# A window-attention layer and three convolution layers: the input laid out ahead of the launch, and the intermediate tensor stored in the layout of its readers

## The chip, the cores and the metric

The kernel runs on one core of a Trainium2 chip. The metric is the device time of one execution in microseconds. Its engines, as the profile names them: PE (TensorE, with PEld for its weight loads), DVE (VectorE), ACT (ScalarE), POOL (GpSimd) and SP (SyncE, which here only issues DMAs). Sixteen DMA engines move the data.

## The reference

The input x has 4 images of 16 channels and 512 x 512 pixels in float32. Four layers follow each other, all with 16 channels in and out:

```python
# layer 0: depthwise 3x3 convolution added to x, then attention in 8x8 windows, then an MLP
x = x + depthwise3x3(x, pos_w) + pos_b
win = windows(x * alpha1 @ color1 + beta1)          # 64 tokens of 16 channels
q, k, v = win @ qkv_w.T + qkv_b                     # 2 heads of 8 channels
x = x + proj(softmax(q * 8**-0.5 @ k.T) @ v)
x = x + fc2(gelu(fc1(x)))                           # 16 -> 64 -> 16
# layer 1: x and weights rounded to 8 bits by their largest value, 3x3 convolution,
#          normalised by mean and variance over all images and pixels, clipped to [0, 6]
# layer 2: x + conv3x3(relu(conv3x3(x, w1) + b1), w2) + b2
# layer 3: x + w2 @ relu(w1 @ conv3x3(x) + b1) + b2 # 16 -> 128 -> 16
```

Two things in it divide the work into stages. Layer 1 can round only when the largest value of all of layer 0's output is known, and it can normalise only when mean and variance of its whole convolution are known. So the output of layer 0 goes to DRAM and is read twice: once for the statistics and once for the real work.

## The kernel before

**Layer 0** is `window_attention`. A tile `x{k}` holds one row of windows (8 pixel rows and a border row above and below) by 128 columns, of 8 strips of each of the 4 images: 128 partitions are image, strip parity and channel (32 b + 16 w + c), and `V = 4` pairs of strips lie along the free dimension. There are 32 such tiles and 64 steps of 64 columns (`STEPS`). `load(k)` (line 271 ff.) brings a tile in with 32 DMAs, one for each image, strip parity and strip pair, each of 16 partitions with 10 rows of 129 or 130 floats; GpSimd sets the borders of the picture to zero. `depthwise` (L297) multiplies it by nine diagonal matrices `taps` (made on DVE at L246 from the constant `hot`), `position` writes the result `y`, and `turn_keys` (L320) transposes blocks of `y` between partitions by 32 DMAs a step into `y2`. `values` (L348), `scores` (L361), `attend` and `divide` are the attention, `project`, `hidden` (L418) and `output` (L431) the rest. In step n, TensorE works on the depthwise convolution of step n + 2 and the hidden layer of step n, and SyncE turns the keys of step n + 1. After each odd step `store` (L447) writes four blocks `xo[:, u]` to DRAM, each with 8 DMAs; `load` of the tile after next is called after each even step. `xo` has one buffer, x tiles two.

The order of PE, DVE, ACT and SP inside layer 0 and inside the convolutions is the order of the program (`tc.manual_schedule`); SP issues its DMAs strictly in that order, and each of its DMAs uses one of eight semaphores in turn, so it waits for the DMA eight places earlier. What stands ahead of the schedule (weights, folding, first constants) is ordered by the framework's scheduler.

At the end of layer 0 a bound on the scores is computed; every engine reads the flag and branches (L133, L539) around `attention_block`, a slower version of layer 0 which doesn't run for this input.

**Layers 1 to 3** are `conv_layers`. Here a tile `tx{mm}` holds one pair of rows of each of four strips (S = 4) of each image: partition is 32 b + 16 (row of the pair) + c, and the free dimension is strip by 512 columns. `_load_pairs` (L898) gathers it from x1 with four DMAs, one for each image, in runs of one row of 512 floats. For mm below 0 or above M = 64 one strip lies outside the picture and is set to zero by DVE. The **statistics pass** goes through the 64 tiles: DVE scales (L990), ACT rounds to bfloat16 (L993), TensorE convolves with the rounded weights (L914), DVE takes the statistics of the four banks (L1015). Loads run four tiles ahead, in four slots; rounding runs two ahead. Then the tiles come a second time, and all four convolutions and layer 3's hidden layer run in one software pipeline, one row pair a turn, in which `turned` (L1101) copies blocks between partitions.

**The tensor between them**, x1, has the shape [image, row + 1, channel, column]; a row of zeros is written above and below each picture at the start (L112, L113).

Of the kernel before, what the change touches and what calls it, by code (L numbers as in the profile page):

```python
# [11 lines left out]
F32 = mybir.dt.float32  # L12
# [11 lines left out]
B, C, H, W = 4, 16, 512, 512  # L24
P = 128
HR = H // 2
WP = W + 2
NS = 8
S = 4
M = H // S // 2  # L30
NH, HD = 2, 8
WS = 8
# [51 lines left out]
        nc.sync.dma_start(part[:, at : at + m, :], src[:, a : a + m, :])  # L84


def _store_rows(nc, dst, src, r0, n):
    for half in range(2):
        a = half * HR + r0 + 1
        for b in range(B):  # L90
            at = 64 * half + C * b
            nc.sync.dma_start(
                dst[b, a : a + n].rearrange("r c w -> c r w"), src[at : at + C]
            )


def _pad_columns(nc, t):
# [1 line left out]


@with_exitstack
def conv_chain(ctx: ExitStack, tc: tile.TileContext, x, mats, vecs, cqs, cws, hots, out):
    nc = tc.nc
    const = ctx.enter_context(tc.tile_pool(name="const", bufs=1))
    dram = ctx.enter_context(tc.tile_pool(name="dram", bufs=1, space=DRAM))


    x1 = dram.tile([B, (S + 1) * 2 * M, C, W], F32, name="x1")
    zero = const.tile([C, W], F32, name="zero")
    nc.vector.memset(zero, 0.0)  # L110
    for b in range(B):
        nc.sync.dma_start(x1[b, 0], zero)  # L112
        nc.sync.dma_start(x1[b, H + 1], zero)  # L113

    mat = const.tile([P, N_MAT], F32, name="mat")
    vec = const.tile([P, N_VEC], F32, name="vec")
    cw = const.tile([P, 3, 2, 3, 32], F32, name="cw")
    nc.sync.dma_start(mat, mats)
    nc.sync.dma_start(vec, vecs)
    nc.scalar.dma_start(cw, cws)  # L120

    def m(name):
        return mat[:, MAT_AT[name]]

    def v(name):
        return vec[:, VEC_AT[name]]

    cq, sw = quant_weights(tc, const, cqs)
    peak = const.tile([P, 4 * HR // WS], F32, name="peak")
    nc.gpsimd.memset(peak, 0.0)  # L130

    safe = window_attention(tc, x, x1, hots, m, v, peak)
    with tc.If(safe == 0):  # L133
        attention_block(tc, x, x1, m, v, peak)
    conv_layers(tc, x1, out, cw, cq, sw, m, v, peak)


@with_exitstack
def window_attention(ctx: ExitStack, tc, x, x1, hots, m, v, peak):

# [10 lines left out]
    nc = tc.nc  # L153
    U = V = 4
# [3 lines left out]
    XW = 2 * BW  # L158
    SR = H // 8
    NQ = W // XW  # L160
# [11 lines left out]
    def quad(i):  # L172
        return slice(32 * i, 32 * i + 32)

    hot = wts.tile([P, 64], F32, name="hot")
    nc.sync.dma_start(hot, hots)
    small, own = hot[:, 0:32], hot[:, 32:64]
# [70 lines left out]
    px = ctx.enter_context(tc.tile_pool(name="w0x", bufs=2))  # L248
# [8 lines left out]
    g = pa.tile([P, V, NJ, NH, T], F32, name="g")  # L257
    o = pa.tile([P, V, NJ, NH, T], F32, name="o")
    most = pa.tile([P, STEPS], F32, name="most")

    def load(k):
        i, cb = divmod(k, NQ)
        t = px.tile([P, V, WS + 2, XW + 2], F32, tag="x", name=f"x{k}")
        if cb == 0:
            nc.gpsimd.memset(t[:, :, :, 0:1], 0.0)
        if cb == NQ - 1:
            nc.gpsimd.memset(t[:, :, :, XW + 1 : XW + 2], 0.0)
        if i == 0:
            nc.gpsimd.memset(t[:, 0, 0, :], 0.0)
        if i == SR // WS - 1:  # L270
            nc.gpsimd.memset(t[:, V - 1, WS + 1, :], 0.0)
        c0, c1 = max(0, XW * cb - 1), min(W, XW * cb + XW + 1)
        at = c0 - XW * cb + 1
        for b in range(U):
            for w in range(2):
                for vv in range(V):
                    r = SR * (2 * vv + w) + WS * i - 1
                    r0, r1 = max(0, r), min(H, r + WS + 2)
                    nc.sync.dma_start(
                        t[32 * b + C * w : 32 * b + C * w + C, vv, r0 - r : r1 - r,  # L280
                          at : at + c1 - c0],
                        x[C * b : C * b + C, r0:r1, c0:c1],
                    )
        return t

    def by_window(ap):
        return ap.rearrange("p (j a x) -> p a j x", a=WS, x=WS)
# [150 lines left out]
    def store(xo, k, u):  # L438
        i, cb = divmod(k, NQ)
        nc.vector.tensor_reduce(  # L440
            peak[:, U * k + u : U * k + u + 1], xo[:, u], AX.XY, ALU.max,
            apply_absolute_value=True,
        )
        for vv in range(V):
            for w in range(2):
                r = SR * (2 * vv + w) + WS * i
                nc.sync.dma_start(  # L447
                    x1[u, r + 1 : r + 1 + WS, :, XW * cb : XW * cb + XW].rearrange(
                        "a c x -> c a x"
                    ),  # L450
                    xo[32 * vv + C * w : 32 * vv + C * w + C, u],
                )

    ctx.enter_context(
# [4 lines left out]
            }  # L459
        )  # L460
    )
    xts, ys = {0: load(0), 1: load(1)}, {}
    for n in range(2):
        for tap in range(9):
            for u in range(U):
# [6 lines left out]
    last, xo = None, None  # L472
    for n in range(STEPS + 1):
# [32 lines left out]
        if n % 2 == 0:  # L506
            xo = px.tile([P, U, WS, XW], F32, tag="xo", name=f"xo{n}", bufs=1)
# [35 lines left out]
def attention_block(ctx: ExitStack, tc, x, x1, m, v, peak):  # L543
# [3 lines left out]
    nc = tc.nc  # L547
# [7 lines left out]
    px = ctx.enter_context(tc.tile_pool(name="l0x", bufs=2))  # L555
# [54 lines left out]
    for i in range(2):  # L610
        t = wts.tile([P, CJ, 4, 2 * C], F32, name=f"vals{i}")
# [137 lines left out]
    def mlp_hidden(xw, n, k, g):  # L749
        xc = chunk(xw, k)  # L750
        ph = psT.tile([P, 4, P], F32, tag="t", name=f"ph{n}_{g}")
        ph = ph.rearrange("p a b -> p (a b)")
        nc.tensor.matmul(
            ph, fc1[32 * g : 32 * g + 32], xc[32 * g : 32 * g + 32], start=True, stop=True
        )
        hid = pa.tile([P, N], F32, tag="hid", name=f"hid{n}_{g}", bufs=3)
        nc.scalar.activation(hid, ph, AF.Gelu, bias=f1b)
        return hid
# [12 lines left out]
    def mlp(xw, i):  # L771

        xo = px.tile([P, WS, W], F32, tag="xo", name=f"xo{i}", bufs=1)
        hids, todo = [], [(k, g) for k in range(NC) for g in range(4)]
        for t in range(len(todo) + 1):
            if t < len(todo):
                k, g = todo[t]
                hids.append(mlp_hidden(xw, f"{i}_{k}", k, g))
            if t:
                k, g = todo[t - 1]  # L780
                if g == 0:
                    pf = psG.tile([P, 512], F32, tag="g", name=f"pf{i}_{k}")
                nc.tensor.matmul(
                    pf[32 * g : 32 * g + 32], m("fc2"), hids.pop(0), start=True, stop=True
                )
                if g == 3:
                    mlp_out(xw, xo, pf, f"{i}_{k}", k)
        nc.vector.tensor_reduce(
            peak[:, i : i + 1], xo, AX.XY, ALU.max, apply_absolute_value=True
        )  # L790
        _store_rows(nc, x1, xo, i * WS, WS)

# [7 lines left out]
    xin, xws, qks, es, ets, os = {0: load(0)}, {}, {}, {}, {}, {}  # L802
# [13 lines left out]
    for at in range(NU + 5):  # L816
        if 0 <= at - 2 < NU:
            _, _, u, n = unit(at - 2)
            ets[at - 2] = turn(es.pop(at - 2), n, u)
        if 0 <= at - 1 < NU:  # L820
            _, _, u, n = unit(at - 1)
            normalise(es[at - 1], n, u)
        if at < NU:
            i, k, u, n = unit(at)
# [3 lines left out]
            if at + 2 < NU:  # L828
                i, k, _, _ = unit(at + 2)
# [5 lines left out]
        if 0 <= at - 3 < NU:  # L835
            i, k, u, n = unit(at - 3)
# [3 lines left out]
        if 0 <= at - 4 < NU and (at - 4) % 4 == 3:  # L840
            i, k, _, n = unit(at - 4)
# [4 lines left out]
        if at < NU:  # L846

            i, k, u, _ = unit(at)
# [36 lines left out]
def _quad(i):  # L885
    return slice(32 * i, 32 * i + 32)


def _load_pairs(nc, t, x1, mm):


    s0, s1 = int(mm < 0), S - int(mm > M)
    if s1 - s0 < S:
        nc.vector.memset(t[:, 0 if mm < 0 else S - 1, :], 0.0)
    at = 2 * M * s0 + 2 * mm
    for b in range(B):
        rows = x1[b, at : at + 2 * M * (s1 - s0)]
        nc.sync.dma_start(  # L898
            t[_quad(b), s0:s1],
            rows.rearrange("(s r) c w -> s r c w", r=2 * M)[:, 0:2].rearrange(  # L900
                "s r c w -> (r c) s w"
            ),
        )


def _turns():
# [316 lines left out]
def _pack(a):  # L1223
# [7 lines left out]
    for w in range(2):  # L1231
# [3 lines left out]
    parts = {  # L1235
        "color1": _diagonal(a["L0_conv_color1"], NS),
        "color2": _diagonal(a["L0_conv_color2"], NS),
        "wq": _diagonal(qkv_w[0].T, NS),
        "wk": _diagonal(qkv_w[1].T, NS),
        "wv": _diagonal(qkv_w[2].T, NS),  # L1240
        "proj": _diagonal(a["L0_conv_proj_w"].T, NS),
        "fc1": np.tile(fc1, (4, 1)),
        "fc2": _diagonal(a["L0_conv_fc2_w"].T, 2),
# [26 lines left out]
    mats = np.concatenate([parts[name] for name, _ in _MATS], axis=1)  # L1270
    vecs = np.concatenate([parts[name] for name, _ in _VECS], axis=1)


    cws = np.zeros((2, C, 4, 2, 3, 2, C), np.float32)
    for i, name in enumerate(
        ("L2_conv_w1", "L2_conv_w2", "L3_conv_conv_w", "L1_conv_weight")
    ):
        w = a[name].transpose(1, 2, 3, 0)
# [6 lines left out]
    cws = np.tile(cws.reshape(32, 4, 2, 3, 32), (4, 1, 1, 1, 1))  # L1285

    own = np.zeros((2, 64, 2, C))
    for w in range(2):
        own[w, :, w, :] = 1.0
    hots = np.concatenate(  # L1290
        [np.tile(np.eye(32), (4, 1)), own.reshape(P, 32)], axis=1
    ).astype(np.float32)
    return {
        "x": a["x"].reshape(B * C, H, W),
        "mats": mats,
        "vecs": vecs,
        "cqs": cws[:, 3].reshape(P, 6 * 32),
# [26 lines left out]
```

## Time and profile before

| | |
|---|---|
| median of 3 runs | 6786.55 us (6781.14 to 6790.85) |
| span of the profiled run | 6787.2 us |
| PE busy | 6456.3 us, 95% |
| ACT, DVE busy | 4215.1 us (62%), 3196.5 us (47%) |
| DMA, mean rate | 76 GB/s, 514.79 MB |
| HBM read, written | 225.28 MB, 134.48 MB |
| loads of a layer 0 tile | 1024 DMAs of about 81 KB |
| stores of layer 0 | 1024 DMAs of 64 KB |
| loads of layers 1 to 3 | 528 DMAs of 256 or 192 KB |

A page of the profile gives the busy time of each engine, then the span in 40 slices (a digit is the busy share of a slice in tenths; PEclk is the clock that TensorE was granted; GB/s is what the DMA engines moved). Further views of the same trace are used below: busy time by stretch, the instructions of one engine in order of time (start, length, engine, line, operation, output<-inputs, and in brackets the idle time ahead and what ended it), and waits by who waited for whom. In the chain that ended last, followed back from the end, only the convolution stage appears (9688 pieces, nearly all TensorE): it reaches back to about 4007 us. What lies before has to be read from the stretches.

The stages by the trace: start until 88 us, layer 0 until 3628 us, statistics pass from 3638 to 3981 us, convolutions to the end.

### The profile page before, as it was taken

Reading aid. Unit: us, or ns where it says so; the run is one execution under the profiler, and the core shown is the slowest. Engines: PE = TensorE matmul, PEld = TensorE weight load, DVE = VectorE, ACT = ScalarE, POOL = GpSimd, SP = SyncE. Lnnn points to the kernel's source line nnn. Section 1 sums busy time; section 2 is a strip of 40 time slices with the busy share of each in tenths; the row PEclk is TensorE's granted clock in tenths of the full one; section 3 lists DMA queues with packets and bytes.
Section 4 is the critical chain, followed back from the end, with each engine's and each line's share of the span. In section 5 each row is a group of like instructions: output and inputs, shape, how many; then the busy total and the mean of one; then the engine's idle time right before and its main releaser. Section 6 shows DMA issues by size and latency. Waiting matters only on the chain. (4 is left out here: it accounts for less than half of the span.)

```text
span 6787.2 us, 317928 instructions
## 1 busy us (share of the span) xinstructions
PE 6456.3 (95%) x146976; PEld 3304.6 (49%) x146976; DVE 3196.5 (47%) x4640; ACT 4215.1 (62%) x5738; POOL 10.3 (0%) x49
## 2 busy tenths in 40 slices
PE   7999999999999999999995569999999999999999
PEld 4555555555555555555552334444444444444443
DVE  2444444444444444444444764444444444444444
ACT  3777777777777777777774344555555555555553
POOL 0000000000000000000000000000000000000000
PEclk9999999999999999999996679999999999999999
DMA  6454555545454545455526962222222222322221
GB/s 72 63 66 65 63 69 63 70 61 69 63 66 62 66 63 66 64 63 68 62 43 131 212 137 72 77 77 78 83 79 78 79 79 79 82 79 78 78 62 46
DMA packets 759438, 514.79 MB, mean 76 GB/s; under 512 B 354128, under 2 KB 648656, under 8 KB 749904
## 3 DMA queue, kind: packets, MB, share of 16 engines
q1 hardware_dynamic: 757808, 493.95, 42.6%
q8 instruction: 1154, 18.91, 1.3%
q14 instruction: 188, 1.54, 0.1%
q10 hardware_dynamic: 288, 0.39, 0.0%
HBM read 225.28 MB, written 134.48 MB: 53 GB/s over the span
## 5 line engine op out<-in xcount | busy, mean ns | idle before, releaser
L1123 PE MATMUL tb<-y,mat 32*32 32x512 f32 x16384 | 1682.9, 597 | 10.4 <-ACT hid L1129 7.5
L1129 ACT ACTIVATE hid<-tb,vec 128x512 f32<-128x512 f32 x1280 | 877.9, 687 | 1229.8 <-PE tb L1123 1207.7
L369 ACT ACTIVATE e<-pair 128x1024 f32<-128x1024 f32 x1024 | 992.4, 1021 | 231.4 <-PE pair L361 230.8
L1131 DVE TENSOR_SCALAR hid<-tb,vec 128x512 f32<-128x512 f32 x768 | 576.6, 751 | 1168.1 <-PE tb L1123 852.8
L297 PE MATMUL pair<-x,taps 32*32 32x512 f32 x18432 | 1005.3, 605 | 35.0 <-issue 20.7
L418 PE MATMUL bank<-y,fc_e 32*32 32x512 f32 x8192 | 890.9, 609 | 10.4 <-issue 6.3
L423 ACT ACTIVATE hid<-bank,f1b 128x512 f32<-128x512 f32 x1024 | 679.6, 686 | 338.3 <-PE bank L418 319.1
L353 DVE COPY yt<-bank 128x512 f32<-128x512 f32 x512 | 353.7, 691 | 906.1 <-PE bank L348 905.8
L1123 PEld LDWEIGHTS tb<-y,mat 32*32 32x32 f32 x16384 | 503.7, 103 | 393.8 <-issue 231.8
L361 PE MATMUL pair<-g,y 32*128 32x128 f32 x16384 | 653.2, 285 | 40.7 <-ACT e L369 36.8
L914 PE MATMUL tb<-z,cw 32*32 32x512 f32 x12864 | 641.3, 602 | 3.5 <-ACT z L1060 2.7
L914 PE MATMUL tb<-q,cq 32*32 32x512 bf16 x12672 | 468.2, 483 | 185.0 <-issue 130.8
L914 PE MATMUL tb<-x,cw 32*32 32x512 f32 x12480 | 635.2, 598 | 1.7 <-ACT z L1060 1.5
L361 PEld LDWEIGHTS pair<-g,y 32*128 32x128 f32 x16384 | 540.3, 187 | 189.3 <-ACT e L369 107.5
L914 PE MATMUL tb<-h,cw 32*32 32x512 f32 x12672 | 628.2, 601 | 1.6 <-ACT z L1060 1.5
L297 PEld LDWEIGHTS pair<-x,taps 32*32 32x32 f32 x18432 | 447.7, 103 | 362.9 <-issue 244.1
L380 PE MATMUL bank<-e,yt 128*32 128x128 f32 x16384 | 555.5, 276 | 1.0 <-ACT r L395 0.9
L385 PE MATMUL bank<-e,hot 128*32 128x512 f32 x4096 | 534.4, 592 | 0.0
L1137 PE MATMUL tb<-hid,mat 128*32 128x512 f32 x4096 | 495.9, 602 | 0.9 <-DVE o L1143 0.9
L380 PEld LDWEIGHTS bank<-e,yt 128*32 128x32 f32 x16384 | 417.7, 109 | 108.5 <-DVE yt L353 52.8
L993 ACT ACTIVATE q<-tx,unround 128x512 bf16<-128x512 f32 (+1 forms) x333 | 313.8, 967 | 235.4 <-DVE tx L990 131.9
L431 DVE TENSOR_TENSOR xo<-bank,y 128x512 f32<-128x512 f32 x256 | 177.0, 691 | 563.8 <-PE bank L429 562.4
(154 smaller groups left out, 6542.0 us busy)
## 6 DMA issues: line engine op xcount, KB each, us to landing
tx<-x SPq DMA_DIRECT2D x520, 256.0 KB, 5.8
y<-y SPq DMA_DIRECT2D x2048, 32.0 KB, 2.1
x<-xo SPq DMA_DIRECT2D x1024, 64.0 KB, 2.1
xi<-x SPq DMA_DIRECT2D x1024, 64.0 KB, 2.6
out_dram<-o SPq DMA_DIRECT2D x64, 1024.0 KB, 4.3
x<-in_x_dram SPq DMA_DIRECT2D x496, 81.2 KB, 6.3
x<-in_x_dram SPq DMA_DIRECT2D x496, 80.6 KB, 6.4
tx<-x SPq DMA_DIRECT2D x8, 192.0 KB, 3.8
```

Of the source, the lines that this page charges most:

```text
L297: nc.tensor.matmul(bank(u)[quad(vv)], taps[quad(u), tap, :], xts[n // 2][quad(u), vv, dy : dy + WS, at : at + BW], start=tap == 0, stop=ta ...
L361: nc.tensor.matmul(bank(u)[:, P * jj : P * jj + P], y2[quad(u), vv, jl + jj].rearrange("p w t -> p (w t)"), g[quad(u), vv, jl + jj].rearra ...
L369: nc.scalar.activation(e[:, 2 * i : 2 * i + 2].rearrange("p u j t -> p u (j t)"), pairs[i], AF.Exp,)
L380: nc.tensor.matmul(b[quad(u), P * jj : P * jj + P], yt[:, jj, quad(u)], e[:, u, jj, :], start=True, stop=True,)
L385: nc.tensor.matmul(d[quad(u)], own, e[:, u].rearrange("p j t -> p (j t)"), start=True, stop=True,)
L418: nc.tensor.matmul(b[quad(k)], fc1[quad(vv), quad(k)], y[quad(vv), u, :], start=True, stop=True,)
L423: nc.scalar.activation(hd, b, AF.Gelu, bias=f1b)
L914: nc.tensor.matmul(p[i][_quad(j)], weights[_quad(i), side, dx, :], src[side][_quad(i), j, dx : dx + W], start=side == 0 and dx == 0, stop= ...
L1123: nc.tensor.matmul(p[_quad(c)], w1[_quad(b), 1 - par, 32 * c : 32 * c + 32], inner(ys(mm + par))[_quad(b), s, :], start=True, stop=True,)
L1129: nc.scalar.activation(hd, p, AF.Relu, bias=v("l3_b1"))
L1131: nc.vector.tensor_scalar(hd, p, v("l3_b1"), 0.0, ALU.add, ALU.max)
L1137: nc.tensor.matmul(out_bank[_quad(b), :], w2[:, par], hd, start=par == 0, stop=par == 1)
```

## The change

Two things are done to the layout of data in DRAM, and one to the order of the first transfers.

The input of layer 0 is laid out ahead of the launch (in `_pack`, with the arrays that hold the weights): xw holds each of the 32 tiles complete, borders and zeros included, so `load` becomes one DMA of 128 partitions with 5200 contiguous floats each, and GpSimd's memsets go. The tile pool moves in front, and the first two loads are written in front of the constant `hot` and all the weight folding. x itself stays as an input for `attention_block`.

x1 gets the layout of the later tiles, [pair, partition, strip, column]. A tile is then one contiguous block of 1 MiB, and `_load_pairs` becomes one DMA (two for the tile mm = M). In exchange the stores of layer 0 have to part even from odd rows: `_store_block` writes two DMAs where there was one, and three where a strip ends and the pair that straddles two strips belongs to the next one.

```diff
+def _store_block(nc, x1, src, b, r0, cols):
+    n = WS // 2
+    s, m = divmod(r0 // 2, M)
+    parts = [(1, m, s, 0, n), (0, m + 1, s, 0, n)]
+    if m + n == M and s < S - 1:
+        parts[1:] = [(0, m + 1, s, 0, n - 1), (0, 0, s + 1, n - 1, 1)]
+    for r, mm, ss, at, k in parts:
+        part = 32 * b + C * r
+        nc.sync.dma_start(
+            x1[mm : mm + k, part : part + C, ss, cols].rearrange("m c x -> c m x"),
+            src.rearrange("c (m r) x -> c m r x", r=2)[:, at : at + k, 1 - r],
+        )
...
-    x1 = dram.tile([B, (S + 1) * 2 * M, C, W], F32, name="x1")
+    x1 = dram.tile([M + 1, P, S, W], F32, name="x1")
...
+    xin = ctx.enter_context(tc.tile_pool(name="w0i", bufs=2))
+    def load(k):
+        t = xin.tile([P, V, WS + 2, XW + 2], F32, tag="x", name=f"x{k}")
+        nc.sync.dma_start(t, xw[k])
+        return t
+    xts, ys = {0: load(0), 1: load(1)}, {}
     hot = wts.tile([P, 64], F32, name="hot")
     nc.sync.dma_start(hot, hots)
...
-    def load(k):
-        i, cb = divmod(k, NQ)
-        t = px.tile([P, V, WS + 2, XW + 2], F32, tag="x", name=f"x{k}")
...
-        for b in range(U):
-            for w in range(2):
-                for vv in range(V):
-                    r = SR * (2 * vv + w) + WS * i - 1
-                    r0, r1 = max(0, r), min(H, r + WS + 2)
-                    nc.sync.dma_start(
-                        t[32 * b + C * w : 32 * b + C * w + C, vv, r0 - r : r1 - r,
-                          at : at + c1 - c0],
-                        x[C * b : C * b + C, r0:r1, c0:c1],
-                    )
...
                 r = SR * (2 * vv + w) + WS * i
-                nc.sync.dma_start(
-                    x1[u, r + 1 : r + 1 + WS, :, XW * cb : XW * cb + XW].rearrange(
-                        "a c x -> c a x"
-                    ),
-                    xo[32 * vv + C * w : 32 * vv + C * w + C, u],
+                _store_block(
+                    nc, x1, xo[32 * vv + C * w : 32 * vv + C * w + C, u], u, r,
+                    slice(XW * cb, XW * cb + XW),
                 )
...
-    xts, ys = {0: load(0), 1: load(1)}, {}
...
 def _load_pairs(nc, t, x1, mm):
-    s0, s1 = int(mm < 0), S - int(mm > M)
...
-    at = 2 * M * s0 + 2 * mm
-    for b in range(B):
-        rows = x1[b, at : at + 2 * M * (s1 - s0)]
-        nc.sync.dma_start(
-            t[_quad(b), s0:s1],
...
+    if mm < 0:
+        nc.vector.memset(t[:, 0], 0.0)
+        nc.sync.dma_start(t[:, 1:S], x1[M + mm, :, 0 : S - 1])
+    elif mm < M:
+        nc.sync.dma_start(t, x1[mm])
+    else:
+        nc.sync.dma_start(t[:, 0 : S - 1], x1[mm - M, :, 1:S])
+        if mm == M:
+            nc.sync.dma_start(t[:, S - 1], x1[M, :, S - 1])
+        else:
+            nc.vector.memset(t[:, S - 1], 0.0)
```

## The prediction

> **What bounds the kernel now.** I read the slices of the span first: they show where TensorE is not the bound. Each of the 40 is about 170 us.
>
> ```profile
> PE   7999999999999999999995569999999999999999
> PEclk9999999999999999999996679999999999999999
> DMA  6454555545454545455526962222222222322221
> GB/s 72 63 66 65 63 69 63 70 61 69 63 66 62 66 63 66 64 63 68 62 43 131 212 137 72 77 77 78 83 79 78 79 79 79 82 79 78 78 62 46
> ```
>
> PE is full except in the first slice and in slices 22 to 24, where DMA reaches its highest share and its highest rate. The busy time by stretch, for the three stages:
>
> ```profile
> core 0: us, PE busy (x) PEld busy (x) DVE busy (x) ACT busy (x) POOL busy (x), PEclk, DMA share, GB/s
> 2000.00:3000.00 1000.00, 980.38 (x21498) 556.59 (x21477) 453.88 (x597) 762.95 (x1016) 1.10 (x6) 1.00 0.53 65
> 3700.00:3900.00 200.00, 107.55 (x3840) 65.10 (x3823) 144.04 (x198) 78.20 (x39) 0.00 (x0) 0.62 1.00 211
> 5000.00:6000.00 1000.00, 1000.00 (x23725) 442.88 (x23727) 481.13 (x764) 506.76 (x764) 0.00 (x0) 1.00 0.29 79
> ```
>
> Layer 0 (98% PE) and the convolution stage (100% PE) are TensorE's; a transfer made cheaper there hides behind matmuls. The statistics pass of layer 1 is different: PE 54%, DVE 72%, ACT 39%, DMA 1.00. It is bound by its loads. Then the start, in SyncE's timeline:
>
> ```profile
> 7.62 0.42 SPq L119 DMA_DIRECT2D vec<-in_vecs_dram  x1
> 10.57 0.35 SPq L176 DMA_DIRECT2D hot<-in_hots_dram  x1
> 24.97 49.54 SPq L279 DMA_DIRECT2D x<-in_x_dram  x64
> 74.96 51.32 SPq L320 DMA_DIRECT2D y<-y  x64
> ```
>
> The 64 loads of the first two tiles wait until 24.97 (on DVE's weight folding) and then hold the queue for 49.54 us; the turns of the first keys stand behind them. PE in the same time:
>
> ```profile
> 31.41 4.34 PE L297 MATMUL pair<-x,taps 32*32 32x512 f32 x8 [6.90 <-DMA x<-in_x_dram]
> ...
> 50.97 9.75 PE L297 MATMUL pair<-x,taps 32*32 32x512 f32 x161 [2.05 <-DMA x<-in_x_dram]
> ...
> 66.64 6.05 PE L297 MATMUL pair<-x,taps 32*32 32x512 f32 x153 [0.88 <-ACT y L308]
> ...
> 88.45 1.11 PE L348 MATMUL bank<-mat,y 128*128 128x128 f32 x4
> ```
>
> It starts at 31.41, stops three times for pieces of x until 50.97, and reaches the first transposes of the attention loop at 88.45. From there it is full.
>
> [...]the packet records give a median of 161 ns for the 2 KiB packets of the statistics loads (12.7 GB/s an engine), 229 ns for the 6016-byte packets of the weights load (26 GB/s) and 314 ns for the 8 KiB packets of the output stores (26 GB/s).[...]
>
> **The change, part by part.**
>
> *Statistics loads.* Four DMAs of 256 KB in 2 KiB runs become one of 1 MiB in 8 KiB runs. From the first scaling at 3645.75 to the end of the last BATCH_NORM at 3980.74 the pass takes 335 us for 64 tiles, 5.2 us each; 1 MiB at 211 GB/s is 5.0 us. The new load: each of 16 engines has 8 packets of 8 KiB. At 314 ns that is 2.5 us a tile[...]. What takes over? Where the loads happened to be early, VectorE's timeline shows the pace without them:
>
> ```profile
> 3802.33 2.49 DVE L1015 BATCH_NORM_STATS2 stats<-tb 128x6 f32<-128x512 f32 x4
> 3804.74 1.27 DVE L990 TENSOR_SCALAR tx<-tx,inv_x 128x2048 f32<-128x2048 f32 x1
> 3806.03 2.49 DVE L1015 BATCH_NORM_STATS2 stats<-tb 128x6 f32<-128x512 f32 x4
> 3808.43 1.27 DVE L990 TENSOR_SCALAR tx<-tx,inv_x 128x2048 f32<-128x2048 f32 x1
> ```
>
> No idle time stands between them: 3.70 us a tile, and VectorE is the new bound (ACT needs 2.0, PE 2.8 at half clock). [...]four tiles are in flight, so the load hides. The pass becomes 64 x 3.70 = 237 us, plus 10 us of ramp (scaling 1.3, rounding twice 2.0, matmuls 2.8, waits): 247. That gives **88 us**. The first tile lands about 4.9 us after its issue (2.5 of data, and the 2.1 us to landing that the smallest issues of the page show) instead of 7.5: 2.6 more. Together **-90 us**, between -60, if bubbles stay, and -95.
>
> *First loads.* Two DMAs of 2.66 MB with a 20.8 KB run for each partition, in SyncE's order between vec and hot. At 26 GB/s on 16 engines a tile takes 6.4 us; issued at 8 and 8.5, both are in by about 22; at half that rate, by 34. Hot (the source of taps) queues behind them and lands with the second. The order of VectorE's instructions moves too: the nine taps operations now all stand after the folding that ends at 24.9, so their wait holds up nothing but themselves. Nine at 0.23 us end at 27; PE can begin at about 26 instead of 31.41, and then has no DMA waits. From 50.97, when the data was there, to 66.64 the first block took 15.7 us; then 21.8 from 66.64 to 88.45. So 26 + 15.7 + 21.8 = 63.5, against 88.45: **-25 us**. I take -24[...] and keep -12 (slow loads) to -30. The turns may start at once, at about 43; eight take 6.4 us (51.32 / 64 each), before the 63 at which they are needed.
>
> *Loads inside layer 0.* 32 issues become one, and the packets of 516 and 520 bytes (88 ns) go; GpSimd's 24 memsets of borders go. All of it lies beside a PE that is 98% busy: nothing.
>
> *Stores of layer 0.* Eight a call become 16 of half the size with the same 512-byte packets; in the bottom row of windows 19, since three strips of eight split once more. SyncE's stores of one pair of steps took 0.475 us an issue, and a zero row of 16 packets takes 0.47 as well: the cost is by issue, not by bytes. In a pair of steps of 110 us the queue has 32 + 64 + 32 = 128 issues now and 1 + 64 + 64 = 129 after. Behind the stores stand the turns of the next step: the stores of 1069.67 to 1089.1 would run to 1103, the turns to 1129, with the next step not before 1142. The slot xo is wanted again at about 1123. Nothing on PE moves. But **the last step has nothing behind which to hide**:
>
> ```profile
> 3609.06 21.99 SPq L447 DMA_DIRECT2D x<-xo  x32
> 3638.26 61.84 SPq L898 DMA_DIRECT2D tx<-x  x55
> ```
>
> VectorE has the flag at 3628.5, SyncE ends its stores at 3631.05, and the next stage loads 7.2 us later, after the branch and the stores' landing. With 76 stores of 0.475 from 3609.06 SyncE ends at 3645.2: **+14 us** on the path (+9 if the smaller stores issue in 0.41).
>
> *Convolution stage.* Four loads a tile become one; PE is at 100%. Nothing. The two memsets of the last tile's strip move; 0.5 us each, hidden.
>
> Sum: 6786.6 - 90 - 24 + 14 = 6686.6; I say **6686**.
>
> **The rivals.** (1) The pass stays at its pace, because something else than the packet size holds it: SyncE's waits in the pass are mostly for a free slot (ACT's rounding), and PE's clock of 0.62 could be the cause rather than the result of waiting. Then only the ends change: 6786.6 - 24 + 14 = 6777. Against it stands the stretch above at 3.70 us a tile; it ran with early loads and a halved clock. (2) Half the gain: VectorE and PE alternate with gaps, some 4.4 us a tile, 282 + 10 us, a gain of 43: 6786.6 - 46 - 24 + 14 = 6731. Stretches of the pass with PE waits of 5.8 us speak for it; they follow late loads, which speaks against. (3) Slower: the new stores step 1 MiB from row pair to row pair. They are 131,072 packets of 512 bytes, 46 ns each at the median now. If that pitch made them eight times as long (370 ns), they would need 131,072 x 0.37 / 16 = 3030 us of the engines, with the turns' 262,144 packets at 28 ns (459 us) and the loads (205 us) some 3690 us, more than layer 0's 3540: +150, for 6786.6 - 90 - 24 + 14 + 150 = 6837. [...]against it the DMA share of 0.53 with half of it to spare.
>
> **How the numbers follow.** The forecast 0.80, the half gain 0.09, the unmoved pass 0.06, the slower case 0.05. The unmoved pass lies within 0.2% (13.6 us) of 6786.6. Faster 0.89, same 0.06, slower 0.05. Range: for the forecast alone, -95 - 30 + 9 gives 6671 and -60 - 12 + 16 gives 6731; the half gain ends there too. I widen a little below, since the ramps are estimates: 6660 to 6735.
>
> **What would show it.** Right: the pass at about 250 us, VectorE there without idle time and DMA's share near a half; the first transposes (in the place of line 348) at 60 to 70 us; SyncE's last store of layer 0 about 19 us behind the last output in place of 5; layer 0's step still some 54 us. Wrong: ACT's rounding still waiting for loads, 8 KiB reads above 450 ns, PE waiting for turned keys, or a DMA share of layer 0 above its 0.53.

## The result, and the profile after

After: **6615.97 us** (median of 4 runs, 6611.96 to 6621.86) against 6787.35 before (4 runs, 6781.14 to 6790.85); ratio 0.9749, interval 0.9732 to 0.9766. That is 171 us less. The forecast was 100 us less, with a range that ended at 6660.

The slices of the page after the change, to be held against those of before (tenths of 40 equal slices; GB/s is what the DMA engines moved):

```profile
PE   8999999999999999999996689999999999999998
...
DMA  3333232333333333333324722222222222222221
GB/s 81 65 67 76 57 75 59 73 60 72 60 72 60 72 61 70 62 70 62 70 44 165 275 85 79 79 79 76 76 78 78 78 78 75 75 79 79 79 63 47
```

TensorE's hole around slices 22 to 24 is shallower and shorter, the highest rate rises from 212 to 275 GB/s, and DMA's share in layer 0 falls from about 5 tenths to 3. The busy time by stretch, with the columns that the prediction's view of the same kind names:

```profile
2000.00:3000.00 1000.00, 988.42 (x21859) 570.83 (x21832) 464.81 (x610) 777.44 (x1036) 0.00 (x0) 1.00 0.32 66
...
3650.00:3750.00 100.00, 67.11 (x2652) 39.24 (x2652) 99.25 (x138) 54.99 (x28) 0.00 (x0) 0.73 0.82 293
```

In layer 0 TensorE is busy 988 us of 1000, where it was 980: that line was expected to stand still. In the statistics pass VectorE is busy 99 us of 100. The start, first on SyncE, then on TensorE (start, length, engine, line, operation; in brackets the idle time before and what ended it):

```profile
7.76 0.90 SPq L194 DMA_DIRECT2D x<-in_xw_dram  x2
```

```profile
24.64 11.38 PE L295 MATMUL pair<-x,taps 32*32 32x512 f32 x288 [0.60 <-DVE taps L269]
37.27 11.71 PE L295 MATMUL pair<-x,taps 32*32 32x512 f32 x288 [1.25 <-ACT y L306]
...
55.22 1.11 PE L346 MATMUL bank<-mat,y 128*128 128x128 f32 x4
```

The two loads are issued at 7.76, TensorE's two depthwise blocks run without a stop, and the first transposes stand at 55.22 (before: 88.45). The seam behind layer 0 on SyncE, 76 stores and then the next stage's first load:

```profile
3516.80 38.39 SPq L96 DMA_DIRECT2D x<-xo  x76
3559.76 37.05 SPq L891 DMA_DIRECT2D tx<-x  x13
```

Put side by side, in us of the profiled executions (the reduction named is the `most` of each step):

| part | before | after | difference | forecast |
|---|---|---|---|---|
| start to the first of the 64 reductions | 108.3 | 75.4 | -32.9 | -24 |
| first to last reduction: layer 0's loop | 3472.4 | 3411.7 | **-60.7** | **0** |
| last reduction to the next stage's first load: the seam | 57.5 | 72.7 | +15.2 | +14 |
| that load to the first scaling | 7.5 | 5.0 | -2.5 | -2.6 |
| statistics pass | 335.0 | 238.7 | -96.3 | -88 |
| the rest (convolution) | 2806.4 | 2814.0 | +7.5 | 0 |

The seam is as forecast. The rest is about scatter: in the eleven experiments that leave the pass and the convolution alone, the same work took 2807.5 to 2813.6. What has to be explained is the loop, and then why start and pass gave more than their terms.

### The profile page after: what moved, and what is told of

Its sections match the earlier page's. It is cut to its first block, busy times and chain, and to the rows that moved or that the text cites. A ratio compares the mean times of both kernels' runs of the same rounds, so it can differ in the third digit from the quotient of the medians.

```text
span 6617.5 us, 317160 instructions
## 1 busy us (share of the span) xinstructions
PE 6388.5 (97%) x146976; PEld 3295.4 (50%) x146976; DVE 3192.7 (48%) x4640; ACT 4209.4 (64%) x5738; POOL 5.9 (0%) x25
## 3 DMA queue, kind: packets, MB, share of 16 engines
q8 instruction: 1154, 18.91, 1.2%
## 5 line engine op out<-in xcount | busy, mean ns | idle before, releaser
L295 PE MATMUL pair<-x,taps 32*32 32x512 f32 x18432 | 968.1, 606 | 1.9 <-ACT y L306 1.3
L908 PE MATMUL tb<-q,cq 32*32 32x512 bf16 x12672 | 446.5, 436 | 122.1 <-ACT q L987 97.9
L378 PEld LDWEIGHTS bank<-e,yt 128*32 128x32 f32 x16384 | 417.7, 109 | 108.1 <-DVE yt L351 52.8
L346 PEld LDWEIGHTS bank<-mat,y 128*128 128x128 f32 x2048 | 215.2, 141 | 430.2 <-issue 376.5
```

Of the source, the lines that this page charges most:

```text
L295: nc.tensor.matmul(bank(u)[quad(vv)], taps[quad(u), tap, :], xts[n // 2][quad(u), vv, dy : dy + WS, at : at + BW], start=tap == 0, stop=ta ...
L378: nc.tensor.matmul(b[quad(u), P * jj : P * jj + P], yt[:, jj, quad(u)], e[:, u, jj, :], start=True, stop=True,)
L908: nc.tensor.matmul(p[i][_quad(j)], weights[_quad(i), side, dx, :], src[side][_quad(i), j, dx : dx + W], start=side == 0 and dx == 0, stop= ...
```

## What the two traces show of the loop

In the trace before, an even step of layer 0 took 56.08 us and an odd one 54.13; after, 54.18 and 54.13. So 1.9 us went from each even step, the one in which x is loaded. By rows of groups over most of the loop (busy us, mean ns, then idle us before and what ended it), before:

```profile
L297 PE MATMUL pair<-x,taps 32*32 32x512 f32 x17568 | 951.2, 603 | 17.0 <-issue 16.7
...
L418 PE MATMUL bank<-y,fc_e 32*32 32x512 f32 x7808 | 848.9, 597 | 6.4 <-issue 6.3
```

and after:

```profile
L295 PE MATMUL pair<-x,taps 32*32 32x512 f32 x17624 | 932.5, 603 | 0.0
...
L416 PE MATMUL bank<-y,fc_e 32*32 32x512 f32 x7960 | 852.4, 600 | 2.0 <-ACT hid L421 1.6 <-DVE y L407 0.4
```

These are the depthwise matmuls and the hidden layer's. Before, TensorE stood 17.0 + 6.4 us ahead of them, ended by "issue": nothing that the profile knows as a wait. After, "issue" is gone from both rows. The page of before names the traffic concerned in its table of queues (packets, MB, share of the engines):

```profile
q8 instruction: 1154, 18.91, 1.3%
```

1154 packets of 16 KB. TensorE executes 293,952 matmuls and weight loads, and with the semaphore instructions among them 295,025, or 256 for each packet: these packets are its instructions, in **blocks of 256**. I number them all in the order of their starts, take the number modulo 256, and call the time from one start to the next a gap. Of the 24 gaps above 1 us in the loop before the change, 21 fall on one and the same value, 193 (the other three lie in the last step). The gaps at that value sum to 63.5 us, where a value's median is 13.4. After, it has 10.7 us, and the median is 8.8. So 52.8 of the 60.7 us lie there; the rest is spread over other places. And each of the 21 gaps ends 1.5 to 2 us after one of these packets has landed. From this I read that TensorE ran out of instructions. Normally (the median after the change) the packet of the next block starts 0.5 us into the present block and lands at 1.6; ahead of the 21 gaps it landed 3.6 to 5.4 us into its block.

## The experiments

The first four test a first version of this theory (A: the small packets of the old loads hold the instruction packets back) and two rivals (B: the stores, or GpSimd's border memsets; C: the number of issues on SyncE). The last column of this table is the sum of gaps at the block boundaries of the loop.

| run | loads of x; when they are issued, us into the even step | loop | gaps at boundaries | time (median) | ratio to before |
|---|---|---|---|---|---|
| before | 32; 19 to 42 | 3472.4 | 63.5 | 6787.4 | 1 |
| after | 1; 34 | 3411.7 | 10.7 | 6616.0 | 0.9749 (0.9732 to 0.9766) |
| e1_x1_only | 32; 45, to 14 of the odd step (medians; later from tile to tile) | 3476.7 | 49.1 | 6697.0 | 0.9866 (0.9849 to 0.9882) |
| e2_xw_only | 1; 19 | 3446.9 | 38.0 | 6739.6 | 0.9934 (0.9918 to 0.9951) |
| e3_short_rows | 1; 34 | 3416.0 | 11.5 | 6621.1 | 0.9755 (0.9739 to 0.9772) |
| e4_32_issues | 32; 34 to 55 | 3416.4 | 31.1 | 6647.3 | 0.9799 (0.9783 to 0.9815) |
| e5_early_load | 1, on ScalarE; 31 | 3561.2 | 18.5 | 6767.1 | 0.9976 (0.9964 to 0.9987) |
| e6_late_load_act | 1, on ScalarE; 36 | 3414.7 | 10.8 | 6620.0 | 0.9752 (0.9735 to 0.9768) |
| e7_xw_only_late | 1, on ScalarE; 36 | 3415.2 | 10.9 | 6707.0 | 0.9876 (0.9860 to 0.9893) |
| e9_sync_k3 | 1; 16 | 3458.7 | 48.7 | 6667.9 | 0.9833 (0.9816 to 0.9849) |
| e10_sync_k5 | 1; 22 | 3432.7 | 24.7 | 6633.4 | 0.9778 (0.9760 to 0.9796) |
| e11_sync_k7 | 1; 29 | 3436.0 | 29.0 | 6641.7 | 0.9789 (0.9770 to 0.9808) |

### Each half of the change alone

e1: the new stores with the old loads (shown against the kernel after).

```diff
-        nc.sync.dma_start(t, xw[k])
+        for b in range(U): ...        # the 32 loads a tile of before, borders by memset
```

> The kernel before with the new x1 alone: its stores, its tiles' loads; x is still loaded by 32 DMAs a tile. Theory A (layer 0's gain of 61 us in its loop comes from the loads of x: their 5120 packets of 516 or 520 bytes keep the DMA engines busy while TensorE fetches its instructions, and it runs dry): the loop from the first to the last of the 64 'most' reductions stays at 3472 us, even steps at 56.1 us, PE starts its loop at 88 us; the statistics pass falls from 335 to 239 us and the seam behind layer 0 grows by 15 us: 6787 - 96 - 3 + 15 + 5 = 6708 us. Rival B (the gain comes from the new stores or from GpSimd): the loop falls to 3412 us and the time to about 6648 us.

The pass got its gain (240.5 us), the loop none (3476.7): the stores do not speed it up. Loads, stores and key turns are now 160 issues for a pair of steps (before 128, after 129), and the loads slip behind the stores into the odd step; a line of TensorE's waits (us in total, times, longest) shows what follows, namely that fc2 waits for VectorE, which waits for the slot that the stores have not freed:

```profile
PE bank L442 <- DVE xo L444: 16.6, 5, 6.4
```

e2: the new loads with the old stores.

```diff
-        _store_block(nc, x1, xo[...], u, r, slice(XW * cb, XW * cb + XW))
+        nc.sync.dma_start(x1[u, r + 1 : r + 1 + WS, :, ...], xo[...])   # as before
```

> The changed kernel with x1, its stores and loads as before; only x is laid out ahead and loaded by one DMA a tile. Theory A: loop 3412 us with even steps at 54.15 us, loop start at 55 us, statistics pass 335 us, no longer seam: 6787 - 33 - 61 = 6693 us. Rival B: the loop stays at 3472 us, 6754 us.

The start is that of after (75.2 us to the first reduction), the pass that of before (341.0). The loop gained 25.5 us of the 60.7 only. No small packet of x is left, the instruction packets take 1.09 us on average (1.12 after), and TensorE still runs dry: 28 of the 38 us of gaps lie 24 to 30 us into the even step. Theory A does not explain that.

### The packets' size, and the number of issues

e3: one load, but in rows of 520 bytes, 5120 packets. e4: 32 loads of 16 partitions each, in rows of 5200 bytes.

```diff
-        nc.sync.dma_start(t, xw[k])
+        nc.sync.dma_start(t, xw[k][:, :, :, 0 : XW + 2])           # e3, rows of P + 4 in DRAM
+        for q in range(8): for vv in range(V):                      # e4
+            nc.sync.dma_start(t[C * q : C * q + C, vv], xw[k][C * q : C * q + C, vv])
```

> The changed kernel, with the rows of xw 132 floats apart in DRAM and 130 of them loaded: still one DMA a tile, but 5120 packets of 520 bytes. Theory A (packets): the even steps lose 1 to 4 us again, the loop takes 3450 to 3530 us, instruction fetches during a load take 1.7 to 2 us again, stalls lie at one place of each 256 TensorE instructions. Rival C (it is the 32 issues of SyncE and their eight semaphores, not the packets): even steps at 54.15 us, loop 3412 us. Under both, the start is longer, since the two first tiles take some 28 us each and hot is behind them: loop start at 90 to 105 us, so under A 6690 to 6780 us, under C 6650 to 6670 us.

> The changed kernel with each tile loaded from xw by 32 DMAs of 16 partitions with 5200 contiguous bytes each: as many issues as before, packets ten times as long. Theory A: even steps at 54.1 to 54.4 us, loop 3412 to 3420 us. Rival C (issues): even steps near 56 us, loop about 3470 us. The start takes some 5 to 20 us more than in the changed kernel, since 64 issues of 0.45 us stand ahead of hot and of the turned keys: 6620 to 6640 us under A, 6680 to 6700 us under C.

Neither brings the loss back. Against A: packets as small as before, at the time of after, cost 4 us. The start came 6 us later than after, and not at the 90 to 105 that I had expected: a 520-byte packet took 31 ns at the median when the load spreads over 128 partitions, 88 ns in the old loads of 16. Against C, 32 issues a tile cost 5 us in the loop (and the start all of its gain, 107.1 us to the first reduction, since 62 more issues stand ahead of all that follows on SyncE). In e4 the gaps at boundaries are 20 us more than after and the loop only 5 us; these gaps lie where ScalarE's exponentials already hold TensorE (offsets 0 to 12 and above 36), which may absorb them; no run tests that.

What e1, e2, e3 and e4 differ in, and what goes with the loss, is **when** the load runs. Theory T, inferred from these times: in a block begun within about 3 us of a load's issue, the instruction packet comes late because of that load's packets, and what is then missing is lost. In e2, for the nine blocks begun 1 to 2 us after the issue, it started 3.2 to 4.6 us into the block and landed 4.1 to 5.5 us into it (medians of after: 0.5 and 1.6). With TensorE going on 1.5 to 2 us after the landing, as at the 21 gaps of before, a packet has to land some 1.5 us before the block ends. The 128 packets of a tile's load take 0.77 us each; in the trace of after it is 8.2 us at the median from the first one's start to the last one's end. Whether the instruction packet waits behind them no run shows: the trace has no record of when it was asked for, and that it waits is argued from the times alone. A block in the attention part lasts 6.1 us, one among the hidden and depthwise matmuls (18 to 36 us into the step) 5.2, and the one that begins there and ends in the next exponentials 7.8. After the change the load is issued 34 us into the step and its burst falls into that long block of 7.8 us. Block by block over the loop, my estimate from these landings, max(0, landing + 1.55 us - length without the gap), follows the measured gaps with a correlation of 0.97 both in before and in e2. Its sums are 41.8 and 32.1 us, where the gaps at the boundaries exceed those of after by 52.8 and 27.3.

### The same load at other times

e6 is the control, e7 the cure for e2, e5 the reverse: the load is issued from ScalarE, behind the fifteenth (e6, e7) or the fifth (e5) hidden activation.

```diff
-        if ahead and n % 2 == 0 and n // 2 + 2 < STEPS // 2:
-            xts[n // 2 + 2] = load(n // 2 + 2)
...
                 hids.append(hidden(y, q, n))
+                if ahead and q == 14 and n % 2 == 0 and n // 2 + 2 < STEPS // 2:   # e5: q == 4
+                    xts[n // 2 + 2] = load(n // 2 + 2, nc.scalar)
```

> The control for the early load: the kernel after, the load issued from ScalarE's queue behind the fifteenth hidden activation, at about 36 us, the time at which SyncE issued it. T and P: loop 3412 (+-6), time 6616 (+-6), nothing from the other queue. If ScalarE's queue itself costs something, it is seen here.

> The kernel before with the numpy layout of the input alone (stores as before), the one load moved from about 19 us of the even step to about 36 us, on ScalarE's queue. T: the 35 us that the loop lost with this part alone (3446.9 against 3411.7) go: loop 3410 to 3420, time 6703 to 6713. Rival B (the old stores are what costs the 35 us): loop 3445, time 6738.

> The kernel after with one thing changed: the one load of an even step is issued from ScalarE's queue behind the fifth hidden activation (about 25 us after the reduction of the step) and not from SyncE's at about 35 us. Same bytes, same packets, same count. Theory T (landing time): TensorE reads its instructions in blocks of 256, [...]it must have landed about 1.6 us before the present one is used up; a load's burst holds the block's packet back to 4 to 5.7 us after the block began, which costs max(0, landing + 1.6 us - length of the block). At 35 us it falls into a block 8 us long and costs nothing; at 25 us it falls into one of 5.3 us: 1 to 2 us in each of 30 even steps, loop 3442 to 3472 us, time 6645 to 6675. Rival P (what is moved counts, not when): loop 3412, time 6616.

e6 is after again within 3 us of the loop (3414.7 against 3411.7), so the other queue itself cost nothing to speak of. **e7 settles e2**: the same bytes, packets and old stores, the load 17 us later, and 31.7 of the 35.2 us that were missing come back. So the new stores speed up the loop only by standing ahead of the load on SyncE: with 64 issues in place of 32 they push it from 19 to 34 us.

e5 does not test T. It lost 150 us, far above what T gives, and its boundaries have only 18.5 us. ScalarE's waits say why:

```profile
ACT hid L421 <- DMA y<-y: 149.9, 28, 10.4
```

ScalarE, which issued the load, stood for DMAs of the key turns that SyncE had sent, 28 times, and the hidden activations stood behind it: 149.9 us, the whole loss. The semaphore numbers in the trace say why. The DMAs of both engines take turns at the same eight semaphores, and a load waits for the DMA that used its semaphore last; in 29 of e5's 30 loads that was a key turn which SyncE had issued only 2.1 to 3.6 us before (a turn lands 2.1 us after its issue at the median). So it is the program's order of semaphores that holds ScalarE; with the same queue and a later load, e6 stood at 3414.7. The load went out at 31 us instead of 25.

So the early placements were made again on SyncE, where no other engine waits: ahead of the second, third and fourth of the step's four groups of key turns.

```diff
+            if k == 3 and n % 2 == 0 and n // 2 + 2 < STEPS // 2:      # e10: 5, e11: 7
+                xts[n // 2 + 2] = load(n // 2 + 2)
             if k % 2 and n + 1 < STEPS:
                 turn_keys(ys[n + 1], k // 2)
```

> The kernel after; the one load of an even step stands on SyncE's queue ahead of the second of the four groups of key turns, where it is issued about 16 us into the step instead of 35. No other engine waits for it there. Theory T (a block of 256 TensorE instructions must have landed about 1.6 us before the block ahead of it is used up[...]): from after's own table of block starts, a load at 15 to 17 us costs 25 to 40 us over the 30 steps. Loop 3437 to 3455, time 6641 to 6660. Rival P (what is moved, not when): loop 3412, time 6616.

> As the run before, but ahead of the third group of turns, about 22 us into the step. T by the same table: at 22 to 23 us only 1.5 to 10 us are lost[...]: loop 3413 to 3425, time 6617 to 6630, clearly less than the placements at 16 and 28 us on either side of it. Rival E (any placement earlier than 32 us collides with the hidden and depthwise matmuls, the more the nearer to them): between the other two or above. P: 3412.

> As the two before, ahead of the last group of turns, about 28 us into the step. T by the same table: 17 to 27 us lost, loop 3430 to 3442, time 6634 to 6647. P: loop 3412, time 6616.

The kernel after with its load 18 us earlier (e9) loses 47 us in the loop, more than three quarters of what the change had gained there. Its two rows, in the view shown above for before and after:

```profile
L295 PE MATMUL pair<-x,taps 32*32 32x512 f32 x17630 | 942.7, 604 | 11.7 <-issue 11.6
...
L416 PE MATMUL bank<-y,fc_e 32*32 32x512 f32 x7835 | 852.6, 598 | 10.2 <-issue 10.2
```

"issue" is back in both. The placement at 22 us loses 21, that at 29 us 24. Of the ranges forecast for the loop, e11's held, e9's ended 4 us too low and e10's 8 us too low. Theory T spoke of blocks begun within about 3 us of the load's issue, and that is too short a reach: in e9, 26 of the 48.7 us of gaps stand behind blocks begun 3 to 6 us after it. At 22 us the table of blocks said 1.5 to 10, and the gaps alone rose by 14; whether 22 us is really better than 29 these runs do not tell, the three microseconds are within the scatter. So rival E of e10's forecast is not excluded as far as it says that every placement ahead of 32 us costs; rival P, by which all three would have stayed at 3412, is. That earlier is not better, and 34 is free, they do.

### The statistics pass: two bounds of one height

e8 leaves the loads alone and halves VectorE's statistics.

```diff
-        for b in range(B):
-            nc.vector.bn_stats(stats[:, mm * B + b, :], p[b])
+        for b in range(2):
+            nc.vector.bn_stats(stats[:, mm * 2 + b, :], p[b])
```

> The kernel after, with the statistics of layer 1 taken from banks 0 and 1 of each tile only: half of the BN_STATS are left out, so the normalisation differs. Tests what the pass stands on now. VectorE (99% busy there, 2.48 us BN_STATS and 1.27 us scaling a tile): the pass falls from 239 us to where the transfers bound it, 64 tiles x 3.75 us x 0.82 busy = 197 us, up to 205; time 6575 to 6583. Rival (the transfers, 0.82 busy and 291 GB/s, are the bound already): the pass stays above 230, time above 6607.

The pass stayed at 241.8 us and the time at 6614.05, on the rival's side of the forecast, but not for the rival's reason. The same stretch of the pass as above:

```profile
3650.00:3750.00 100.00, 59.50 (x2623) 39.30 (x2626) 67.75 (x83) 54.13 (x27) 0.00 (x0) 0.81 0.78 289
```

VectorE 68, DMA 0.78: neither is full. TensorE's waits over the pass (us in total, times, longest) are, in before, after and e8:

```profile
PE tb L914 <- issue: 130.3, 41, 6.0
```

```profile
PE tb L908 <- issue: 18.7, 20, 2.3
```

```profile
PE tb L908 <- issue: 80.1, 44, 3.6
```

TensorE starves here too. At the block boundary (in this stage on another value of the number modulo 256, 36) its gaps sum to 155.5 us of the pass before, 31.9 after, and 101.7 in e8. And VectorE in e8 waits for TensorE, hardly ever for a load:

```profile
DVE stats L1009 <- PE tb L908: 79.6, 47, 4.1
DVE tx L984 <- DMA tx<-x: 5.8, 3, 3.5
```

So the loads do not hold the pass through their data; while VectorE's busy time in this stretch fell from 99 to 68 us, TensorE's gaps at the boundary rose from 31.9 to 101.7. The line of before was there to be read, and I had read its waits as late loads.

e12 halves the loads as well: 512 KB a tile in place of 1 MiB.

```diff
-            load(mm + 4, tags[mm % 2])
+            loaded[mm + 4] = loaded[mm]
+            nc.sync.dma_start(loaded[mm][:, 0:2], x1[mm + 4, :, 0:2])   # and scaled() of strips 0:2
```

> The kernel with half of the BN_STATS left out (which stood at 242 us in the pass, TensorE stopping 102 us at its instruction blocks), and with half of the loads of its statistics pass left out too: from the fifth tile on only strips 0 and 1 are loaded (64 tiles of 512 KB in 4 KB runs) and scaled, the other two keep the data of the first tiles. TensorE, ScalarE and the BN_STATS have the same work as there. Theory T: the burst ahead of an instruction block is half as long, so the block lands about 1.2 us earlier; TensorE's stops fall from 102 to 35 to 60 us and the pass to 175 to 200 us. Rival V (TensorE's own pace at the granted clock, or ScalarE, holds the pass): 230 to 242, unchanged.

```profile
3650.00:3750.00 100.00, 65.81 (x3009) 42.92 (x2992) 60.08 (x93) 60.51 (x31) 0.00 (x0) 0.81 0.52 170
```

```profile
PE tb L908 <- issue: 64.1, 43, 3.3
```

The pass fell to 215.3 us, the time to 6587.93, and TensorE's gaps at the boundary to 85.2. The direction is T's. Of the fall that I expected, the pass shows about half and the gaps about a third; so some 10 us of the pass's fall are not explained by the gaps. (VectorE's scaling is halved with the loads, but VectorE was not full in e8.) The estimate had no floor. Between two boundaries the shortest usual time is 3.5 us: in such blocks the packet starts 1.1 us in, lands at 2.1 and TensorE goes on 1.4 us later. From these times I estimate that part of the gap would stay without any burst; no run of the pass is without loads.

### The seam, on two queues

```diff
-        nc.sync.dma_start(
+        (nc.scalar if other and (r == 0 or other[1]) else nc.sync).dma_start(
...
+                    (0, u == 2) if k == STEPS // 2 - 1 and u >= 2 else None,
```

> The kernel after; of the last step's 76 stores the 19 of u=2 and half of those of u=3 are issued from ScalarE's queue, which has no more activations to do there, the rest from SyncE as before. If the 15 us that the seam grew by are SyncE's 0.47 us an issue and nothing else, SyncE ends 28 issues or 13 us sooner (3539 in place of 3552 in after's trace), close behind the flag at 3536, and the stretch from the last reduction of layer 0 to the next stage's first load falls from 72.7 to 57 to 61 us: time 6600 to 6606. Rival (the stores' landing in the new layout takes longer, or the branch sets the end): 70 to 73 us, time 6616.

```profile
3511.58 32.01 SPq L96 DMA_DIRECT2D x<-xo  x46
```

```profile
3525.70 17.51 ACTq L96 DMA_DIRECT2D x<-xo  x30
```

```profile
SPq L96 <- DMA x<-xo: 9.8, 4, 8.9
```

The time was 6606.96 us (5 runs, 6605.67 to 6614.25), ratio to before 0.9746 (0.9733 to 0.9759); the interval overlaps that of after, so that it beats after is not shown. In the profiled run the seam fell from 72.7 to 65.0 us, about half of what the issues alone would give. SyncE's 46 stores end at 3543.6 with the flag at 3531: in the middle of the last eight it stood 9 us for an earlier store to land (the third view), a wait that took the place of the issues removed. It is again the program's: the store that stood until 3540.5 shares its semaphore with one that ScalarE had issued only at 3539.0.

## Why the prediction was wrong

*"Loads inside layer 0 ... All of it lies beside a PE that is 98% busy: nothing."* **This is the step that failed.** It was worth 60.7 us. A PE that is 98% busy was taken to have nothing to gain, and it had: its instructions came by DMA too (q8: 1154 packets, 1.3% of the 16 engines' time), and it stood where these packets landed late, 3.6 to 5.4 us into the block instead of 1.6. Only part of that shows in the missing 2%. By the two rows of before, the depthwise and hidden matmuls had 23 us of "issue" in front of them; from start to start, the gaps at the block boundaries were 52.8 us longer than after. Much of the rest is counted as busy: a matmul counts for 0.6 us (603 ns on average), though in a full stream one starts every 0.05 us (951.2 us for 17,568), so about the first 0.6 us of each stop does not show (the three stops shown below last 1.6, 2.3 and 2.0 us from start to start, and 0.96, 1.67 and 1.40 us in the view). Removing the small loads is 25.5 us of it (e2), moving the one load to where its burst does no harm the other 35.2 (e7 regained 31.7, e9 to e11 lose 21 to 47 of the 60.7 again).

*"Stores of layer 0 ... Nothing on PE moves."* Wrong for the same reason: the longer row of stores moves the load, and the load moves TensorE. The stores' own cost was rightly put at nothing: a 512-byte packet took 40 ns after, 46 before, and rival 3 (the 1 MiB pitch) did not occur.

*Start, -24.* Measured -32.9. TensorE began at 24.64, where 26 was said. The term that was mis-sized is the length of the two depthwise blocks, 15.7 and 21.8 us taken over from before: they took 12.6 and 17.95. In before, TensorE's timeline has three stops that the sum carried along:

```profile
61.69 4.07 PE L297 MATMUL pair<-x,taps 32*32 32x512 f32 x103 [0.96 <-issue]
...
74.36 4.52 PE L297 MATMUL pair<-x,taps 32*32 32x512 f32 x128 [1.67 <-issue]
80.28 0.63 PE L297 MATMUL pair<-x,taps 32*32 32x512 f32 x4 [1.40 <-issue]
```

They are gaps of 1.6, 2.3 and 2.0 us from start to start, all three at number 193 modulo 256, the first two beside the second tile's small loads, the third beside the turns that followed them.

*Statistics loads, -88 and -2.6.* Measured -96.3 and -2.5. The 8 KiB reads took 309 ns at the median (361 on average), where 314, the median of the output stores before, was taken; VectorE is full, and the tile takes 3.7 us, as forecast. (In the stretch of before from which the 3.70 us were read, 3802 to 3815 us, the granted clock was 0.50.) The term that was mis-sized is the ramp: 10 us were added to the 237 of 64 tiles, and the pass took only 2 more. The reason given for before, that the pass is bound by its loads, was at most part of it. DMA's share was 1.00, but VectorE's waits over the pass before were

```profile
DVE stats L1015 <- PE tb L914: 84.8, 36, 5.8
DVE tx L990 <- DMA tx<-x: 19.9, 7, 6.4
```

It stood for TensorE four times as long as for a load, while TensorE had 155.5 us of gaps at its block boundaries. The loads filled the DMA engines and TensorE stood at its blocks at the same time; how much each of the two cost in before no run separates.

*Seam, +14.* Measured +15.2, by the issue time of 0.47 us that was used; e13 confirms the cause in part. *Convolution stage, nothing:* within the scatter.

The signs that were named as right appeared, except that the first transposes came at 55 and not at 60 to 70, and that DMA's share of the pass stayed at 0.82 and not "near a half". The step of layer 0 is indeed "some 54 us"; what I had not read is that it was 55.1 on average before, 56.08 in the even steps beside 54.13 in the odd ones. Asking why they differ would have led to the block boundaries.

## What to carry to other kernels

When idle time of an engine is put down to "issue", look for its instruction packets among the DMA queues and for the engine's gaps by instruction number modulo the block: here a load that was off every data path went with 52.8 us of such gaps in a long unrolled loop. Then the place of a large load in time can matter as much as its shape: issued 34 us into the step, where the instruction block lasted 7.8 us, it was free, and at 16 us it cost 47; and moving other issues on the queue moved it (64 stores in place of 32, from 19 to 34 us). Do not take an engine that is 98% busy to have nothing to gain (here 60.7 us of 3472.4). And before relieving the engine that is full, look for a second limit just below it (e8: VectorE from 99 to 68 us of 100, the pass unchanged at 241.8).

## What the runs showed of the hardware

- Before: 1154 packets of 16 KB on the instruction queue for 295,025 TensorE instructions, 256 for each, and 21 of the loop's 24 gaps above 1 us at one value of the number modulo 256. At the median a packet started 0.5 us into the block ahead of its own and landed at 1.6 (after).
- An instruction packet took 1.0 us at the median where no load of x ran, 1.8 beside the old loads (before; 1.7 to 1.9 ahead of the 21 gaps). TensorE went on 1.3 to 1.8 us after a late one had landed (medians of the runs). The shortest usual time for a block was 3.5 us, in the statistics pass.
- Beside a load of 2.66 MB in 20,800-byte packets (0.77 us each), the instruction packet of a block begun 1 to 3 us after the load's issue started 3.2 to 4.7 us into that block (e2; median of after: 0.5).
- 520-byte rows took 31 ns a packet in one DMA over 128 partitions (e3), 88 ns in DMAs over 16 partitions (before); 5200-byte rows over 16 partitions took 662 ns (e4), 20,800-byte rows over 128 partitions 773 ns (after).
- TensorE's busy share showed a part of its stops only: it rose from 980 to 988 us of 1000, 8 in 1000, while the loop became 60.7 of 3472.4 us shorter, 17 in 1000.
- With two issuing engines, one stood for the other's DMAs: ScalarE up to 10.4 us at a load (e5), SyncE 8.9 us at a store (e13). In both cases the DMAs of the two engines shared eight semaphores, which is a matter of the program.
